# Spreading a layernorm's factors with one rounded product on a diagonal of blocks, in a local-attention feed-forward

## The chip, the cores and the metric

The kernel runs on one core of a Trainium2 chip, as one program. The metric is device time in microseconds of one execution; runs of the same kernel on the chip give a median. Engines are named as in the profile: PE multiplies matrices (PEld is its loading of weights), DVE is the vector engine, ACT the scalar engine, POOL the GpSimd engine, and SP issues the transfers. Each engine works through its own instructions in order and waits at semaphores for the others.

## The reference

The reference is a chain of eight blocks with residuals on x of 8 x 256 x 128 (batch, tokens, features): a state-space block, a local transformer, a softmax attention, the same local transformer again, a linear attention, a quantised feed-forward, a head attention, the quantised feed-forward. The change lies in the local transformer, which the kernel runs twice, six layers each time:

```python
for i in range(DEPTH):
    x = attn_layer(shift_tokens(x), Wqkv[i], q_scale[i], k_scale[i], Wo[i]) + x
    x = ffn_layer(shift_tokens(x), ln_g[i], ln_b[i], W1[i], b1[i], W2[i], b2[i]) + x

def ffn_layer(x, g, bln, W1, b1, W2, b2):
    mu = x.mean(-1, keepdims=True)
    var = ((x - mu) ** 2).mean(-1, keepdims=True)
    xn = (x - mu) / jnp.sqrt(var + 1e-05) * g + bln
    hg = xn @ W1 + b1
    a, gate = jnp.split(hg, 2, -1)
    return a * jax.nn.gelu(gate, approximate=False) @ W2 + b2
```

The attention has 16 heads of 64, windows of 32 tokens that look at themselves and the one before, l2-normed queries and keys, and rotary factors. The layernorm at the head of `ffn_layer` is what the change touches.

## The kernel before

Features lie on the 128 partitions and tokens along the free dimension. The batch is cut into four chunks of 512 tokens (two sequences of 256). A local-transformer stage (`LocalBlock`) has 6 layers x 4 chunks = 24 units; a unit goes through 8 steps, one for each pair of heads. `steps` writes out one order by hand for all engines, with the tile scheduler off: step i does, for several units at once, the part of each that is due. The names of a step, in the order in which they are issued:

- what the list `top` holds from the step before (small POOL subtractions of `split`, L203);
- `rotate`, POOL, two passes over 128x1024, L367 and L368, of the pair projected in the step before, after SP has swapped its halves;
- `prep`, PE L410 and twice DVE L414: the keys times their rounded factors `rs`;
- `attend`, PE L505, `share`, DVE L460 and L461, and `project`: PE `mm3` (L213 to L215), ACT copies L338 and squares L348, DVE L340;
- `rounded`, twice a unit: ACT L397, POOL L398, PE transposition L401, ACT L403; it makes the `rs` that the next step's `prep` multiplies by;
- `shared`, POOL L469; then weight loads that are due (`load_v` PE L283, `load_1` PE L296, ACT L298, DVE L299, L301);
- `norms` and `norms_end`: ACT L131 to L134, DVE L377, L142, L146, twice a unit;
- one piece of `feed`, the feed-forward of an older unit, in seven pieces and an eighth in the last step;
- `attended`, `turn` (PE L482, ACT L485), then what the list `mid` holds;
- `scores`: PE L429, then four DVE passes L437 to L440; `values`: PE L325, ACT L327; `squares`: PE L359; and `soft`: ACT's exponent L450, over the pair of scores that DVE has just finished, in odd steps.

The layernorm of `feed` is `layernorm_in_pieces`, cut over three steps. Piece one centres x with a matmul (L159), squares it (L161) and copies it (L163). Piece two sums the squares into `var`, where 32 rows of each quarter of the tile hold the variance of one quarter's 128 tokens (L167); ACT makes the first guess of the inverse root (L131, L132, L134), and `newton` is put on the list `mid`, so that DVE corrects it (L144, L146) later in the same step, ahead of that step's scores. Its result `y[0]` is 128x128: rows 32s to 32s+31 hold the factors of tokens 128s to 128s+127, all rows alike. Piece three, in the next step, spreads them over 128 partitions into the 128x512 bank `rb`, with four fp32 matmuls whose weights `one[:, s]` are 1 in row 32s and 0 elsewhere (L179); then DVE multiplies (L541). Each fp32 matmul appears in the trace as two records. Piece three falls into a step in which `rounded` runs too.

fp32r is fp32 rounded for a matmul of one pass; where full precision is needed, the kernel splits a value into a rounded part and the rounded rest (`split`, L203). Tiles of fp32r live in an arena of their own. PSUM has eight banks: five (RING) go round, and scores, norms and the attention's sum have one each.

Of the kernel before, what the change touches and what calls it, by code (L numbers as in the profile page):

```python
# [10 lines left out]
F32 = mybir.dt.float32  # L11
F32R = mybir.dt.float32r
BF = mybir.dt.bfloat16
AF = mybir.ActivationFunctionType
ALU = mybir.AluOpType
# [22 lines left out]
RING, SCO, NRM, ACC = "01234", "5", "6", "7"  # L38
# [5 lines left out]
def f32(ap):  # L44
    return ap.bitcast(F32)


class Arena:
# [3 lines left out]
    def __init__(self, big, at=0, end=SIZE, rounded=None):  # L52
        self.big, self.at, self.end, self.tags, self.rounded = big, at, end, {}, rounded
# [33 lines left out]
class K:  # L87
# [64 lines left out]
            pass  # L152
        return xs, rb

    def layernorm_in_pieces(self, pool, src, tags, sfx="", deep=2, mid=None):

        nc = self.nc
        xc = self.bank(tags[0])
        nc.tensor.matmul(xc, self.cmat, src, start=True, stop=True)  # L159
        sq = pool.tile([128, CT], F32, name="lnsq", tag="sq" + sfx, bufs=deep)  # L160
        nc.scalar.activation(sq, xc, AF.Square)  # L161
        xs = pool.tile([128, CT], F32, name="lnx", tag="fx" + sfx, bufs=deep)
        nc.scalar.activation(xs, xc, AF.Copy, scale=-0.5)  # L163
        yield xs, None
        var = self.bank(tags[1])
        for s in range(4):
            nc.tensor.matmul(var[32 * s:32 * s + 32, 0:128], self.ones32, sq[:, bass.ts(s, 128)],  # L167
                             start=True, stop=True)
        t = self.rsqrt_tables(pool, var, bias=self.eps, sfx=sfx)
        y = []  # L170
        newton = lambda: y.append(self.rsqrt_newton(pool, var, t, bias=self.eps, sfx=sfx))
        if mid is None:
            newton()
        else:
            mid.append(newton)
        yield xs, None
        rb = self.bank(tags[1])
        for s in range(4):
            nc.tensor.matmul(rb[:, bass.ts(s, 128)], self.one[:, s], y[0], start=True, stop=True)  # L179
        yield xs, rb  # L180

# [36 lines left out]
class LocalBlock:  # L218


    def __init__(self, k):
        self.k, self.nkb = k, 0
        nc = k.nc
        R = Arena(k.bigr, 0, RSIZE)
        self.P = P = Arena(k.big, k.con.at, SIZE, R)
        self.D = k.D
        self.mask = k.const(P, "c_mask", (128, 512), BF)
        self.hcol = k.const(P, "c_hcol", (128, 2))
        self.sel = k.const(P, "c_sel", (128, 2, GP, 32))
        bsel = P.tile([128, GP, 128], F32, name="c_bsel", tag="rr", bufs=1)  # L230
        nc.sync.dma_start(out=bsel, in_=k.a["c_bsel"])
        self.bsel = P.tile([128, GP, 128], F32R, name="bsel")
        nc.vector.tensor_copy(self.bsel, bsel)
        self.qs = k.const(P, "qs", (128, DEPTH, 4))
        self.ffc = k.const(P, "lngb", (128, DEPTH, 2))
        self.b2 = k.const(P, "b2", (128, DEPTH))
        self.b1 = k.const(P, "b1", (128, DEPTH, 6))
        self.zero = P.tile([32, 128], BF, name="zero")
        self.kb = [P.tile([128, 2, 32 + CT], F32, name="kb_%d" % i) for i in range(NKB)]
        self.y = [P.tile([128, 2, 257], F32, name="y_%d" % c) for c in range(NCH)]  # L240
        for t in [self.zero] + self.kb + self.y:
            nc.vector.memset(t, 0.0)

        for tag, n, bufs in (("fx", 512, 2), ("sq", 512, 3), ("lny", 128, 2), ("nwt128", 128, 2),
                             ("tab0", 512, 2), ("tab1", 512, 2), ("wr_64", 512, NWR), ("wr_128", 256, NWR),
                             ("wvo", 512, NWV), ("bias1", 8, 2), ("w2", 128, 3)):
            P.place(tag, n, bufs)
        for tag, n, bufs in (("xs", 1024, 2), ("wqk", 512, 9), ("w1", 256, 7), ("fh", 1024, 1), ("rs", 512, 2)):
            R.place(tag, n, bufs)

        self.rs, self.nrs = [P.tile([128, CT], F32R, name="rs", tag="rs") for _ in range(2)], 0
        for t in self.rs:
            nc.vector.tensor_scalar(t, self.mask, 0.0, None, ALU.mult)
# [280 lines left out]
    def feed(self, u):  # L534
        k, P, nc, w = self.k, self.P, self.k.nc, u.w
        assert u.att
        for xc, rb in k.layernorm_in_pieces(P, self.y[u.c][:, :, 0:256], (RING, RING), mid=self.mid):
            if rb is None:
                yield
        xn = P.tile([128, CT], F32, name="xn", tag="fx", bufs=2)  # L540
        nc.vector.tensor_tensor(xn, xc, rb, ALU.mult)  # L541
        yield
        xh = k.split(P, xn, (128, CT), "fh", 1, self.top)
        yield
        ge = P.tile([128, 3, CT], F32, name="ge", tag="ge", bufs=1)
        for i, m in enumerate((128, 128, 85)):
            gp = k.bank(RING)
            k.mm3(gp[:m], w.w1[3 + i], xh)
            nc.scalar.activation(ge[:m, i], gp[:m], AF.Gelu, bias=w.bias1[:m, 3 + i:4 + i])
        u.late = True  # L550
        yield
        yield
        hh = []
        for i, m in enumerate((128, 128, 85)):
            ap = k.bank(RING)
            k.mm3(ap[:m], w.w1[i], xh)
            nc.vector.scalar_tensor_tensor(ge[:m, i], ap[:m], w.bias1[:m, i:i + 1], ge[:m, i], ALU.add, ALU.mult)
            hh.append(ge[:m, i])
        yield
        acc = k.bank(RING)  # L560
        for i in range(3):
            m = (128, 128, 85)[i]
            nc.tensor.matmul(acc, w.w2[i][:m], hh[i], start=(i == 0), stop=(i == 2))
        self.residual(u.c, acc, self.b2[:, u.l:u.l + 1])
        yield
# [40 lines left out]

    def steps(self, us, ws, depth):
        NU, done, feed, side = len(us), [0] * NCH, None, []
        for i in range(-LEAD, 8 * NU + 20):
            def do(what, ahead):  # L610
# [26 lines left out]
            if 0 <= n < NU:  # L637
                u = us[n]
                last = u.l + 1 == depth
                if p == 0:  # L640
                    feed, fed = self.feed(u), u
                if p < 7:
                    next(feed)
# [856 lines left out]
```

## Time and profile before

| | before |
|---|---|
| runs, median (lowest to highest) | 4365.39 us (4363.03 to 4368.97), n = 3 |
| the profiled execution | 4360.81 us, span 4359.0 us, granted clock 0.926 |
| PE, DVE, ACT, POOL busy, share of the span | 87%, 85%, 60%, 71% |
| L179, PE | 480 records, 0.275 us each (median), all layernorms together |
| L367 and L368, POOL | 384 each, 2.39 us each |
| L437 to L440, DVE | 384 each, 0.69 to 0.70 us each |
| L450, ACT | 192, 1.06 us each |

How to read it: the page gives busy times over the whole span, the span in 40 slices, and groups of instructions by line. A window table gives busy times of a stretch, a timeline the instructions in order of time with start and duration, and in square brackets the idle time before an instruction and what ended it. An arrow `out<-in` names what is written and read: `big` and `bigr` are the two arenas in SBUF, `pb` is PSUM. Matmuls overlap in their pipe, so what one costs PE is read from the start of one to the start of the next. The local stages lie between some 690 and 2180 us and between 2470 and 3990 us; the state-space stage comes before, and attention stages between and behind.

### The profile page before, as it was taken

How to read it: one execution, taken by the hardware profiler on the slowest of the kernel's cores; microseconds unless marked ns; L12 is line 12 of the kernel's file. 1: busy time of each engine (PE TensorE's matmuls, PEld its weight loads, DVE VectorE, ACT ScalarE, POOL GpSimd, SP SyncE). 2: the span in 40 equal slices, each digit the busy share in tenths (PEclk: the TensorE clock that was granted, in tenths of full speed). 3: DMA queues.
4: the chain of work that ended last, by engine and by line, in shares of the span. 5: the costliest groups of instructions: out<-in, count | busy, mean ns of one | idle time of the engine just before them, and what ended most of it. 6: DMA issues, size and time to landing. Idle time of an engine off the chain costs nothing. (4 is left out here: it accounts for less than half of the span.)

```text
span 4359.0 us, 147963 instructions
## 1 busy us (share of the span) xinstructions
PE 3780.3 (87%) x64201; PEld 2852.4 (65%) x64201; DVE 3716.3 (85%) x5687; ACT 2628.5 (60%) x5050; POOL 3077.8 (71%) x1546
## 2 busy tenths in 40 slices
PE   5666679999999999999966899999999999998367
PEld 2222248777878778787744788787787877875144
DVE  6999958888888888888976788888888888897988
ACT  5433347777667676676645676676676767764322
POOL 3656668877778787787566887787787877872433
PEclk7777889999999999999977999999999999998578
DMA  0000023323233233232202332232323323321000
GB/s 19 7 3 16 1 77 78 91 73 89 73 74 89 71 89 76 71 93 71 63 22 67 81 92 74 69 94 72 89 70 76 87 71 90 75 72 47 15 6 10
DMA packets 134900, 272.98 MB, mean 63 GB/s; under 512 B 31020, under 2 KB 68328, under 8 KB 134248
## 3 DMA queue, kind: packets, MB, share of 16 engines
q1 hardware_dynamic: 134248, 263.51, 24.0%
q8 instruction: 504, 8.26, 0.8%
q14 instruction: 148, 1.21, 0.1%
HBM read 49.50 MB, written 6.29 MB: 13 GB/s over the span
## 5 line engine op out<-in xcount | busy, mean ns | idle before, releaser
L367 POOL TENSOR_TENSOR big<-big 128x1024 f32<-128x1024 f32 x384 | 915.8, 2385 | 466.7 <-DMA big<-big 322.6
L368 POOL TENSOR_TENSOR big<-big 128x1024 f32<-128x1024 f32 x384 | 916.5, 2387 | 30.1
L325 PE MATMUL pb<-big 128*32 128x128 f32 x24576 | 748.1, 274 | 2.7 <-DVE big L301 2.7
L325 PEld LDWEIGHTS pb<-big 128*32 128x32 f32 x24576 | 683.0, 111 | 8.5 <-DVE big L301 4.0
L327 ACT COPY big<-pb 128x512 f32<-128x512 f32 x768 | 439.4, 597 | 384.2 <-PE pb L325 381.0
L338 ACT COPY big<-pb 128x512 f32<-128x512 f32 x768 | 437.5, 587 | 276.8 <-PE pb L215 241.7
L414 DVE SCALAR_TENSOR_TENSOR big<-big,pb 128x512 f32<-128x512 f32 x768 | 536.0, 738 | 22.3 <-PE pb L410 22.0
L340 DVE TENSOR_TENSOR big<-pb,big 128x512 f32<-128x512 f32 x768 | 496.4, 677 | 58.6 <-ACT big L338 51.5
L213 PE MATMUL pb<-bigr 128*128 128x512 f32 (+1 forms) x1056 | 453.9, 430 | 9.8 <-DVE big L340 4.3
L469 POOL TENSOR_TENSOR big<-big 128x1024 f32<-128x1024 f32 x192 | 365.6, 1904 | 132.2 <-ACT big L338 54.8
L348 ACT ACTIVATE big<-big 128x512 f32<-128x512 f32 x768 | 444.2, 631 | 0.0
L821 POOL TENSOR_TENSOR big<-big 128x1024 f32<-128x1024 f32 x128 | 305.1, 2396 | 192.1 <-DVE big L820 187.1
L429 PE MATMUL pb<-big 128*32 128x128 f32 x12288 | 421.3, 278 | 6.0 <-DVE big L440 6.0
L215 PE MATMUL pb<-bigr 128*128 128x512 f32 (+1 forms) x1056 | 422.2, 400 | 4.6 <-DVE bigr L299 4.6
L214 PE MATMUL pb<-bigr 128*128 128x512 f32 (+1 forms) x1056 | 420.9, 399 | 1.1 <-POOL bigr L203 1.1
L429 PEld LDWEIGHTS pb<-big 128*32 128x32 f32 x12288 | 316.6, 110 | 142.2 <-issue 91.2
L437 DVE TENSOR_TENSOR pb<-pb,big 128x512 f32<-128x512 f32 x384 | 266.3, 694 | 144.2 <-PE pb L429 142.6
L505 PE MATMUL pb<-big 128*32 128x128 f32 x11520 | 377.9, 276 | 0.2 <-ACT big L485 0.2
L814 PE MATMUL pb<-bigr 128*128 128x512 f32 x512 | 216.1, 538 | 181.3 <-DVE big L820 125.7
L450 ACT ACTIVATE big<-big 128x1024 f32<-128x1024 f32 x192 | 203.7, 1061 | 263.6 <-DVE big L440 261.9
L505 PEld LDWEIGHTS pb<-big 128*32 128x32 f32 x11520 | 325.1, 110 | 48.0 <-issue 25.0
L816 ACT ACTIVATE big<-pb,big 128x1020 f32<-128x1020 f32 x128 | 142.2, 1111 | 282.0 <-PE pb L814 191.1
(270 smaller groups left out, 7450.7 us busy)
## 6 DMA issues: line engine op xcount, KB each, us to landing
big<-big SPq DMA_DIRECT2D x768, 256.0 KB, 3.6
big<-in_wqk SPq DMA_DIRECT2D x96, 128.0 KB, 3.5
big<-x SPq DMA_DIRECT2D x28, 256.0 KB, 2.7
big<-in_c_rot SPq DMA_DIRECT2D x24, 256.0 KB, 5.1
big<-in_wv SPq DMA_DIRECT2D x48, 128.0 KB, 3.6
big<-in_wo SPq DMA_DIRECT2D x48, 128.0 KB, 4.0
big<-big SPq DMA_DIRECT2D x384, 16.0 KB, 2.2
x<-big SPq DMA_DIRECT2D x20, 256.0 KB, 2.5
```

Of the source, the lines that this page charges most:

```text
L213: mm(out, w[:, 0], x[:, 0], start=start, stop=False)
L215: mm(out, w[:, 1], x[:, 0], start=False, stop=stop)
L325: nc.tensor.matmul(vp[32 * h:32 * h + 32, bass.ts(w, 128)], xw, wv[:, bass.ts(h, 128)], start=True, stop=True)
L327: nc.scalar.copy(v2[:, 4 * q:4 * q + 4].rearrange("p w f -> p (w f)"), vp)
L338: nc.scalar.copy(raw[:, s], ps)
L340: nc.vector.tensor_tensor(tt[:, s].rearrange("p (b t) -> p b t", b=2), ps.rearrange("p (b t) -> p b t", b=2), ct, ALU.mult)
L348: nc.scalar.activation(sq, raw[:, s], AF.Square)
L367: nc.gpsimd.tensor_tensor(s4, s4, u.w.tab[1][:, :, None, :].broadcast_to([128, 2, 2, T]), ALU.mult)
L368: nc.gpsimd.tensor_tensor(tt, tt, sw, ALU.add)
L414: nc.vector.scalar_tensor_tensor(kb[:, h, 32:], tt[:, 1], self.hcol[:, h:h + 1], rb, ALU.mult, ALU.mult)
L429: mm(s4[32 * w:32 * w + 32, 2 * wg:2 * wg + 2], qf[:, 32 * win:32 * win + 32], kb[:, :, 32 * win:32 * win + 64].rearrange("p h (o j) -> p ...
L505: mm(u.acc[32 * w:32 * w + 32, bass.ts(wg, 128)], pts[o][:, 32 * win:32 * win + 32], v2[:, win - 1 + o], start=False, stop=(g == 3 and o = ...
```

## The change

In the feed-forward's layernorm alone (`feed` passes `top`; other layernorms stay), the four fp32 matmuls L179 become one fp32r matmul over 512 columns. For that `newton`, on DVE, gets three more 128x128 passes: `hi` is the rounded `y[0]`; then `y[0]` is scaled by column 0 of `part` and has `hi` times column 1 added, so that row 32s holds the rounded value, row 32s+1 the rest, and the others 0. Four ACT copies, put on `top` and so issued at the head of the next step, write `y[0]` times column 2+s of `part` into quarter s of `z` (128x512, fp32r), which leaves two rows of each quarter: a diagonal of blocks. The weights `two` have 1 in rows 32s and 32s+1. The tiles `part` and `two` are set up once, with 26 small memsets and one cast on DVE. Line numbers below L179 move by 30 or less: in the changed kernel the three DVE passes are L179 to L181, the ACT copies L184, the new matmul L194.

```diff
+        def newton():
+            y.append(self.rsqrt_newton(pool, var, t, bias=self.eps, sfx=sfx))
+            if top is None:
+                return
+            hi = pool.tile([128, 128], F32R, name="lnh", tag="lnh")
+            nc.vector.tensor_copy(hi, y[0])
+            nc.vector.tensor_scalar(y[0], y[0], self.part[:, 0:1], None, ALU.mult)
+            nc.vector.scalar_tensor_tensor(y[0], f32(hi), self.part[:, 1:2], y[0], ALU.mult, ALU.add)
+            z = pool.tile([128, 4, 128], F32R, name="lnz", tag="lnz", bufs=2)
+            for s in range(4):
+                top.append(lambda s=s: nc.scalar.activation(z[:, s], y[0], AF.Copy, scale=self.part[:, 2 + s:3 + s]))
+            y.append(z.rearrange("p s t -> p (s t)"))
...
-        for s in range(4):
+        if top is not None:
+            nc.tensor.matmul(rb, self.two, y[1], start=True, stop=True)
+        for s in range(4 * (top is None)):
             nc.tensor.matmul(rb[:, bass.ts(s, 128)], self.one[:, s], y[0], start=True, stop=True)
...
+        two = P.tile([128, 128], F32, name="two", tag="rr", bufs=1)
+        nc.vector.memset(two, 0.0)
+        k.part = P.tile([128, 6], F32, name="part")
+        nc.vector.memset(k.part, 0.0)
+        for s in range(4):
+            nc.vector.memset(two[32 * s:32 * s + 2], 1.0)
+            nc.vector.memset(k.part[32 * s:32 * s + 2, 0:1], 1.0)
+            nc.vector.memset(k.part[32 * s:32 * s + 1, 0:1], 0.0)
...
+        k.two = P.tile([128, 128], F32R, name="two")
+        nc.vector.tensor_copy(k.two, two)
...
-        for xc, rb in k.layernorm_in_pieces(P, self.y[u.c][:, :, 0:256], (RING, RING), mid=self.mid):
+        for xc, rb in k.layernorm_in_pieces(P, self.y[u.c][:, :, 0:256], (RING, RING), mid=self.mid, top=self.top):
```

More of the change, by code (lines that the diff above doesn't have):

```diff
@@ L153, in layernorm, with layernorm_in_pieces @@
         return xs, rb
-    def layernorm_in_pieces(self, pool, src, tags, sfx="", deep=2, mid=None):
+    def layernorm_in_pieces(self, pool, src, tags, sfx="", deep=2, mid=None, top=None):
         nc = self.nc
@@ L170, in layernorm_in_pieces @@
         y = []
-        newton = lambda: y.append(self.rsqrt_newton(pool, var, t, bias=self.eps, sfx=sfx))
+        def newton():
[10 more added lines that the diff above has]
+            y.append(z.rearrange("p s t -> p (s t)"))
         if mid is None:
@@ L242, in __init__ @@
             nc.vector.memset(t, 0.0)
+        two = P.tile([128, 128], F32, name="two", tag="rr", bufs=1)
[6 more added lines that the diff above has]
+            nc.vector.memset(k.part[32 * s:32 * s + 1, 0:1], 0.0)
+            nc.vector.memset(k.part[32 * s:32 * s + 2, 1:2], -1.0)
+            nc.vector.memset(k.part[32 * s:32 * s + 1, 1:2], 1.0)
+            nc.vector.memset(k.part[32 * s:32 * s + 2, 2 + s:3 + s], 1.0)
+        k.two = P.tile([128, 128], F32R, name="two")
+        nc.vector.tensor_copy(k.two, two)
         for tag, n, bufs in (("fx", 512, 2), ("sq", 512, 3), ("lny", 128, 2), ("nwt128", 128, 2),
```

## The prediction

> **What bounds the kernel now.** I read the page's busy times, then the stage table (windows), then the timeline of all engines around one feed step.
>
> ```profile
> PE 3780.3 (87%) x64201; PEld 2852.4 (65%) x64201; DVE 3716.3 (85%) x5687; ACT 2628.5 (60%) x5050; POOL 3077.8 (71%) x1546
> ...
> PE   5666679999999999999966899999999999998367
> ```
> ```profile
> 1000.00:1900.00 900.00, 874.07 (x17339) 702.42 (x17340) 779.00 (x1233) 631.64 (x1205) 707.38 (x357) 1.00 0.33 81
> ```
>
> In 900 us of local attention PE is busy 874 us (97%) at the full clock, DVE 87%, POOL 79%, ACT 70%. Nearly all of PE's 26 idle us are waits for DVE or a late transfer. So in these two stages (about 690 to 3990 us) a microsecond taken from PE is won, and one in which PE stands is lost. The change acts in the step after the one where `newton` runs. An ordinary one, with chunk 3 in the feed-forward (timeline; start, duration):
>
> ```profile
> 1454.07 0.29 DVE L146 SCALAR_TENSOR_TENSOR big<-big,pb 128x128 f32<-128x128 f32 x1
> ...
> 1454.28 0.69 DVE L437 TENSOR_TENSOR pb<-pb,big 128x512 f32<-128x512 f32 x1
> ...
> 1455.10 2.38 POOL L367 TENSOR_TENSOR big<-big 128x1024 f32<-128x1024 f32 x1 [0.96 <-DMA big<-big]
> ...
> 1456.46 0.69 DVE L440 TENSOR_TENSOR big<-pb,big 128x512 f32<-128x512 f32 x1
> ...
> 1457.24 1.06 ACT L450 ACTIVATE big<-big 128x1024 f32<-128x1024 f32 x1 [1.65 <-DVE big L440]
> ...
> 1458.21 1.09 ACT L338 COPY big<-pb 128x512 f32<-128x512 f32 x2
> ...
> 1458.51 0.27 PE L401 MATMUL pb<-big 128*128 128x128 f32 x1
> 1458.62 1.06 PE L179 MATMUL pb<-big 128*128 128x128 f32 x8
> ...
> 1459.61 1.08 PE L429 MATMUL pb<-big 128*32 128x128 f32 x32
> ...
> 1460.98 1.28 POOL L398 TENSOR_TENSOR bigr<-big,bigr 32x512 fp32r<-32x512 f32 x1 [1.04 <-ACT big L403]
> ...
> 1462.80 0.50 PE L410 MATMUL pb<-bigr 128*128 128x512 f32 x1
> ```
>
> Call T the end of the layernorm's L146 (1454.36 here). PE has already finished this step's scores, so DVE is the late one: it goes straight from L146 to the scores' four passes (L437 to L440, done at T+2.79). ACT's exponent L450 has waited 1.65 us for them and ends at T+3.95. PE meanwhile is at prep, attend and projections, and reaches L179 at T+4.2 without a wait, since its operand is four microseconds old. The next scores start at T+5.25.
>
> **PE, removed and added.** L179 holds PE from 1458.62 to 1459.61, 1.0 us (1.1 in other feeds). One 128x512 fp32r matmul takes its place: such matmuls stand 0.23 us apart in a row (L213 to L215) and 0.33 to 0.43 us before another kind (L410). I take 0.38. Saved: some 0.65 us in each of 48 feeds, 31 us if nothing else moved.
>
> **DVE, added.** Three 128x128 passes between L146 and L437, each waiting for the one before. The 128x128 copy at L195 took 0.21 us; the shortest one-source scalar pass of that kind (L1168) 0.21; the nearest two-source pass is L299, 0.35 at its quick end. With 0.03 between them: d = 0.87 us if nothing blocks them.
>
> **ACT, added, and the new wait.** Four 128x128 scaled copies into fp32r. L1035, a 128x128 pass, lasts 0.39 and starts every 0.29, so four take about 1.27. They stand at the head of the next step, which on ACT's queue is behind L450, and L450 waits for L440. So z is complete at T + 3.95 + d + 1.18 (they may start 0.1 before L450 ends, as L338 does). The new matmul waits for z, and behind it on PE wait the next scores, values and everything else. New start of L429: T + 3.95 + 0.87 + 1.18 + 0.05 for the signal + 0.38 = T+6.43, against T+5.25 for chunks 0 and 3 (1.2 us lost), T+5.07 for chunk 1 (1.4 lost), and T+6.51 for chunk 2, where L283 stands ahead of L179 (0.1 won). 12 feeds of each: 14 + 16 + 14 - 1, about **+43 us**, the matmul's saving already in it. Bounds: if z were never late, -31; if the four copies ran end to end at 0.39, 0.35 more per feed, +17.
>
> **Behind it on ACT**: L338, L348, L397 and L403 run without gaps there, so all slip by d + 1.18 = 2.05, and so does POOL's L398, which makes the factors that the next step's first matmul L410 reads. L398 would end at T+9.95; L410, before at T+8.44, would come at T+9.6. Another 0.4 us in chunks 0, 1 and 3, 0.2 in chunk 2: **+16** (from 0 to 25). ACT has about 2.4 idle us a step, so that slip is gone in two steps.
>
> **Blocked by POOL.** Two instructions on SBUF alone do not pass each other on DVE and POOL in this trace. L299's shortest run is 0.31 us, its median 1.1, and it ends 0.1 to 0.15 us after the POOL instruction that it met. Two such passes in a row show it best:
>
> ```profile
> 2101.82 2.38 POOL L367 TENSOR_TENSOR big<-big 128x1024 f32<-128x1024 f32 x1 [3.98 <-PE pb L429]
> ...
> 2102.39 5.13 DVE L587 TENSOR_TENSOR big<-big 64x512 f32<-64x512 f32 x2
> ...
> 2104.28 2.69 POOL L368 TENSOR_TENSOR big<-big 128x1024 f32<-128x1024 f32 x1
> ```
>
> Two passes of 0.67 us each took 5.13: the first until L367 ended, the second until L368 did. L146 and the scores' passes have a PSUM operand and run through. The three new passes have none. One-source passes are held too: L692 takes 0.28 us, and 0.81 where it met POOL. I went through the 46 feeds that have scores behind them: in 20 POOL is idle at T and L367 comes only at T+0.6 to T+1.1 or later, when the last pass has begun, so d stays 0.87. In 26 (nine of chunk 0, where L299 had made T late, all twelve of chunk 1 with its L203, five of chunk 3) an L367, L368 or L203 is running, and another often follows at once. Letting DVE and POOL alternate as above gives d between 1.0 and 6.1 there, 2.7 more than free on average: 26 x 2.7 = **+70 us**. Bounds: +8 by the same table if only the two-source pass is held, 0 if the phases shift clear of POOL; all 35 feeds of chunks 0, 1 and 3 at 3.5 more, +123. I take 70, by L587 and L692.
>
> The Trainium skill (VectorE: DVE Perf Modes, the perf-mode tier table; SBUF — State Buffer, two separate sides) says that fp32 copies and scalar passes in SBUF run at twice the rate by taking both read ports, and then lock POOL out or wait for its whole instruction, as two-input passes do. L692 agrees for the scalar pass; no run here shows the 128x128 copy against POOL. By the rule all three passes alternate with POOL, and the sum would be the one below; without it for the copy and the scalar pass the sum would be some 60 us less.
>
> **Once, at the start**: 27 small memsets and copies on DVE during the state-space stage, where DVE is busy 500 of 560 us. At 0.06 us for one (L112), 2 us. The instruction order there and in the stage between shifts a little; I give that 5 us either way. **Given back**: feeds of chunks 0 and 1 already have 2 to 5 us in which PE waits for a late DVE; a PE that was held for z finds DVE less late. I take -8 (0 to -25).
>
> **Sum**: 43 + 16 + 70 + 2 - 8 = 123. The profiled execution took 4360.8 us (span 4359.0); its sum is 4484. The median of the runs is 4.6 higher, inside the noise of this term, so I forecast 4484, 2.8% slower.
>
> **Rivals.**
> 1. *The saving wins.* If L450 or the copies were done by T+4.2, PE would have its 0.65 us each time: 4361 - 31 = 4330. That needs DVE to have a slack of 2 us at T, and L437 starting right behind L146 with PE's scores 1.8 us old speaks against it. It decides as soon as z is ready before L401 ends. Chance 5%.
> 2. *Only the wait.* POOL's instructions shift so that the three passes fall into gaps, or the one-source passes are not held: 4361 + 43 + 16 + 2 + (0 to 8) - 8, 4414 to 4422. For it: PE's new stalls move DVE's and POOL's phases every feed. Chance 22%.
> 3. *More collisions.* DVE delayed, POOL's rotations bunch up, and the free feeds collide too: up to 4361 + 43 + 16 + 123, about 4543. For it: POOL is 79% busy and L367 comes only 0.75 us after T in many free feeds. Chance 13%.
> 4. *Gain and loss cancel*, PE waiting 0.65 us each time: 4361. Chance 3%. The forecast itself, 4430 to 4520: 57%.
>
> **How the numbers follow.** About 0.2% is what a measurement of this kernel can tell from no change. Faster is rival 1 (0.05), the same is rival 4 (0.03), all the rest is slower (0.92). The range runs from rival 2, with 10 us for the shifted order, to just short of rival 3's end: 4405 to 4535.
>
> **What would show it.** Right: a group of 48 matmuls at the new line with an idle time before it of 1 to 5 us, released by ACT's scaled copies, 80 to 150 us in all, PE's share in local attention down by 2 to 3 points. Right on the collisions: the three DVE lines with medians over their minima of 0.2 to 0.35 us and maxima near 2.4. Wrong: no idle time ahead of the new matmul (rival 1), or DVE lines all at their minima (rival 2). Idle PE ahead of L410 released by L398 would confirm the 16.

## The result, and the profile after

The changed kernel takes 4517.47 us (median of 4 runs, 4509.65 to 4534.91) against 4364.21 us for the kernel before: ratio 1.0357, 95% interval [1.0339, 1.0376]. The profiled execution took 4523.8 us, span 4522.0, granted clock 0.912 (before 0.926). The forecast was 4484 us with a range to 4535; by medians the change costs 153 us where the sum said 123.

The page's busy times and PE's strip, after:

```profile
PE 3814.3 (84%) x63865; PEld 2850.4 (63%) x63865; DVE 3844.9 (85%) x5858; ACT 2679.3 (59%) x5242; POOL 3078.8 (68%) x1546
...
PE   5666679999999899999966899999999999987367
```

The window table of 1000 to 1900 us (after the times: busy us of PE, PEld, DVE, ACT and POOL, then granted clock, DMA share, GB/s):

```profile
1000.00:1900.00 900.00, 828.72 (x16168) 659.53 (x16169) 777.73 (x1204) 606.35 (x1181) 661.71 (x332) 0.97 0.31 74
```

In the same 900 us PE is busy 829 us, 92%, instead of 874, and its clock is 0.97 instead of 1.00: there is less work done in the window, and some of it runs slower. DVE is as busy as it was, since its new passes fill what the slower pace leaves.

PE's waits after (us in total, times, longest):

```profile
PE pb L194 <- ACT bigr L184: 149.7, 48, 8.7
...
PE pb L440 <- POOL bigr L428: 18.2, 28, 5.6
```

The new matmul L194 waits in each of its 48 executions, always for the copies L184. Prep's matmul (L440, before L410) waits for POOL in 28 cases where it was 8; the added ones are short, about 0.2 us each. Before, the line was:

```profile
PE pb L410 <- POOL bigr L398: 15.5, 8, 6.9
```

A feed of chunk 1 shows how the wait comes about (timeline; all lines after moved by 30, so scores are L467 to L470 on DVE, the exponent L480, the rotation L397 and L398):

```profile
1072.72 0.29 DVE L146 SCALAR_TENSOR_TENSOR big<-big,pb 128x128 f32<-128x128 f32 x1
...
1073.05 0.73 DVE L179 CAST bigr<-big 128x128 fp32r<-128x128 f32 x1
...
1073.81 2.50 DVE L180 TENSOR_SCALAR big<-big 128x128 f32<-128x128 f32 x1
1073.84 2.38 POOL L397 TENSOR_TENSOR big<-big 128x1024 f32<-128x1024 f32 x1 [0.15 <-DVE bigr L179]
...
1076.30 2.36 POOL L398 TENSOR_TENSOR big<-big 128x1024 f32<-128x1024 f32 x1
1076.35 2.46 DVE L181 SCALAR_TENSOR_TENSOR big<-bigr,big 128x128 f32<-128x128 f32 x1
...
1078.73 0.69 DVE L467 TENSOR_TENSOR pb<-pb,big 128x512 f32<-128x512 f32 x1
...
1081.69 1.06 ACT L480 ACTIVATE big<-big 128x1024 f32<-128x1024 f32 x1 [7.44 <-DVE big L470]
1082.66 1.26 ACT L184 ACTIVATE bigr<-big 128x128 fp32r<-128x128 f32 x4
...
1083.97 0.80 PE L194 MATMUL pb<-bigr 128*128 128x512 f32 x1 [6.74 <-ACT bigr L184]
...
1084.70 1.94 PE L459 MATMUL pb<-big 128*32 128x128 f32 x32
```

A scaled pass over 128x128 (L180) takes 2.50 us and ends with POOL's L397; L181 ends just after L398. The scores' first pass L467 starts 5.7 us after T (the end of L146) instead of 0.89 as in a feed that meets no POOL instruction (before, it started 0.08 ahead of T), and the exponent, the copies, the matmul and the scores follow in a chain. PE stands 6.74 us. Over all 48 layernorms the three passes lasted (shortest, median and longest, in ns, behind the count):

```profile
L179 DVE CAST bigr<-big x48: 216/294/2382, 728.7 to 4167.1; 128x128 fp32r<-128x128 f32 x48
L180 DVE TENSOR_SCALAR big<-big x48: 274/288/2502, 729.0 to 4168.6; 128x128 f32<-128x128 f32 x48
L181 DVE SCALAR_TENSOR_TENSOR big<-bigr,big x48: 336/351/2544, 729.3 to 4169.7; 128x128 f32<-128x128 f32 x48
```

Behind PE's stand the scores L459 last 1.94 us where they took 1.08 before. That was not in the forecast; the window table of these microseconds shows why:

```profile
1075.00:1080.00 5.00, 2.24 (x24) 1.45 (x16) 4.93 (x4) 0.00 (x0) 3.58 (x2) 1.00 0.03 7
1080.00:1087.00 7.00, 3.03 (x49) 2.44 (x53) 6.44 (x11) 5.11 (x12) 0.45 (x1) 0.51 0.14 31
1087.00:1090.00 3.00, 3.00 (x81) 2.62 (x70) 2.90 (x5) 1.69 (x3) 2.92 (x3) 1.00 0.90 232
```

The granted clock fell to 0.50 at 1080.08, in the stand, for 6.83 us, and so past its end. In the local stages, all 22 stands of PE of 4 us or more are followed or met by such a drop of 3.41 or 6.83 us; of the 18 between 1.5 and 3 us only 6 are. But 4 us are no threshold: the kernel before has no such stand there, and 8 of its 12 stands between 1.5 and 3 us met a drop of 3.41 us.

A yardstick for what follows: I call **stretch** the time from a feed's first score pass on DVE (L437 before) to the next feed's. The last one of each local stage ends at the stage's last first pass. There are 46 in the local stages, of one chunk each; a feed's own wait for z lies in its own stretch, and the next feed's DVE passes lie in it too. Sums of stretches by chunk, in us, from the profiled executions (the names are those of the experiments below):

| | chunk 0 | chunk 1 | chunk 2 | chunk 3 | sum |
|---|---|---|---|---|---|
| before | 830.2 | 779.1 | 662.7 | 652.5 | 2924.5 |
| after | 882.2 | 824.7 | 676.7 | 702.9 | 3086.5 |
| e1, DVE passes alone | 860.8 | 788.7 | 670.7 | 687.6 | 3007.8 |
| e2, ACT copies alone | 844.0 | 791.5 | 662.2 | 661.5 | 2959.2 |
| e3, matmul alone | 825.8 | 776.5 | 657.0 | 650.3 | 2909.6 |
| e5, early copies | 861.4 | 790.5 | 667.5 | 690.9 | 3010.3 |
| e9, filled stand of chunk 1 | 872.3 | 808.7 | 673.4 | 707.6 | 3062.0 |
| e10, both remedies, ring turned | 838.8 | 790.1 | 662.1 | 660.1 | 2951.1 |
| e11, the same with two passes | 838.5 | 787.3 | 659.3 | 657.6 | 2942.7 |

The stretches hold 162 us of the 163 by which the span grew: all of the loss is in the two local stages.

### The profile page after: what moved, and what is told of

Same layout as the page of the kernel before. It is cut to its first block, busy times and chain, and to the rows that moved or that the text cites. A ratio compares the mean times of both kernels' runs of the same rounds, so it can differ in the third digit from the quotient of the medians.

```text
span 4522.0 us, 147661 instructions
## 1 busy us (share of the span) xinstructions
PE 3814.3 (84%) x63865; PEld 2850.4 (63%) x63865; DVE 3844.9 (85%) x5858; ACT 2679.3 (59%) x5242; POOL 3078.8 (68%) x1546
## 4 chain that ended last, share of the span: by engine, by line
PE 44%; DVE 30%; ACT 14%; issue 7%; POOL 4%; DMA 2%; SPq 0%; POOLq 0%; ACTq 0%; DVEq 0%
PE pb L355 8%; PE pb L459 5%; PE pb L535 5%; DVE big L850 4%; PE pb L230 4%; PE pb L232 3%; PE pb L231 3%; PE pb L593 3%; ACT big L368 2%; ACT big L378 2%; PE pb L389 2%; PE pb L440 2%; DVE big L370 2%; PE pb L512 2%; DVE pb L468 2%
## 5 line engine op out<-in xcount | busy, mean ns | idle before, releaser
L397 POOL TENSOR_TENSOR big<-big 128x1024 f32<-128x1024 f32 x384 | 915.6, 2384 | 467.9 <-DMA big<-big 287.6
L398 POOL TENSOR_TENSOR big<-big 128x1024 f32<-128x1024 f32 x384 | 916.1, 2386 | 30.1
L355 PE MATMUL pb<-big 128*32 128x128 f32 x24576 | 769.7, 279 | 4.1 <-DVE big L331 3.9
L355 PEld LDWEIGHTS pb<-big 128*32 128x32 f32 x24576 | 704.0, 113 | 13.2 <-DVE big L331 6.1
L357 ACT COPY big<-pb 128x512 f32<-128x512 f32 x768 | 438.3, 596 | 384.1 <-PE pb L355 381.8
L444 DVE SCALAR_TENSOR_TENSOR big<-big,pb 128x512 f32<-128x512 f32 x768 | 536.1, 739 | 30.1 <-PE pb L440 29.9
L459 PE MATMUL pb<-big 128*32 128x128 f32 x12288 | 438.6, 286 | 9.9 <-DVE big L470 9.7
L480 ACT ACTIVATE big<-big 128x1024 f32<-128x1024 f32 x192 | 203.8, 1061 | 382.0 <-DVE big L470 380.2
L459 PEld LDWEIGHTS pb<-big 128*32 128x32 f32 x12288 | 328.5, 114 | 156.8 <-issue 95.1
L467 DVE TENSOR_TENSOR pb<-pb,big 128x512 f32<-128x512 f32 x384 | 266.7, 694 | 155.8 <-PE pb L459 154.0
L535 PE MATMUL pb<-big 128*32 128x128 f32 x11520 | 379.6, 276 | 0.5 <-issue 0.3
L535 PEld LDWEIGHTS pb<-big 128*32 128x32 f32 x11520 | 325.9, 110 | 49.5 <-issue 26.8
```

The lines of the kernel that those rows point to most:

```text
L355: nc.tensor.matmul(vp[32 * h:32 * h + 32, bass.ts(w, 128)], xw, wv[:, bass.ts(h, 128)], start=True, stop=True)
L397: nc.gpsimd.tensor_tensor(s4, s4, u.w.tab[1][:, :, None, :].broadcast_to([128, 2, 2, T]), ALU.mult)
L398: nc.gpsimd.tensor_tensor(tt, tt, sw, ALU.add)
L444: nc.vector.scalar_tensor_tensor(kb[:, h, 32:], tt[:, 1], self.hcol[:, h:h + 1], rb, ALU.mult, ALU.mult)
L459: mm(s4[32 * w:32 * w + 32, 2 * wg:2 * wg + 2], qf[:, 32 * win:32 * win + 32], kb[:, :, 32 * win:32 * win + 64].rearrange("p h (o j) -> p ...
L535: mm(u.acc[32 * w:32 * w + 32, bass.ts(wg, 128)], pts[o][:, 32 * win:32 * win + 32], v2[:, win - 1 + o], start=False, stop=(g == 3 and o = ...
```

## Experiments: the parts alone

The theory was that of the forecast: DVE's three passes held up by POOL, and the matmul's wait for z behind the exponent, which stands on ACT's queue ahead of the copies. Each part was first put into the kernel alone. Two rivals: the parts cost their own length only, and the saving on PE is lost in other waits.

**e1: the three DVE passes alone**, their results used by nobody; the old four matmuls stay.

```diff
-            nc.vector.tensor_scalar(y[0], y[0], self.part[:, 0:1], None, ALU.mult)
-            nc.vector.scalar_tensor_tensor(y[0], f32(hi), self.part[:, 1:2], y[0], ALU.mult, ALU.add)
+            w = pool.tile([128, 128], F32, name="lnt", tag="lnt")
+            nc.vector.tensor_scalar(w, y[0], self.part[:, 0:1], None, ALU.mult)
+            nc.vector.scalar_tensor_tensor(w, f32(hi), self.part[:, 1:2], w, ALU.mult, ALU.add)
```

> Of the change only the three DVE passes are left: they write into tiles that nobody reads, and the four fp32 matmuls spread the factors as before. Lock theory: a pass on SBUF alone waits for POOL's whole instruction, so in about 25 of 46 feeds the scores' passes come 3 to 6 us late and PE waits for the next keys; the free feeds stay inside DVE's slack of 1.1 us. Before + 66 us + some 10 us of lowered clock after long stands: about 4440 (4415 to 4465), the three lines with maxima near 2.4 us. Rival, mere length: three passes of 0.3 us lie inside the slack, 4364 to 4372, and no maximum above 0.5.

Measured: 4449.33 us, ratio 1.0193 [1.0177, 1.0208], against 4363.02 in the same series. More than half of the change's loss comes from three passes of 0.2 to 0.35 us that nobody waits for but DVE's own queue.

**e2: the four ACT copies alone**, at the head of the next step, reading the factors that are there; results unused.

```diff
-            hi = pool.tile([128, 128], F32R, name="lnh", tag="lnh")
-            nc.vector.tensor_copy(hi, y[0])
-            nc.vector.tensor_scalar(y[0], y[0], self.part[:, 0:1], None, ALU.mult)
-            nc.vector.scalar_tensor_tensor(y[0], f32(hi), self.part[:, 1:2], y[0], ALU.mult, ALU.add)
...
-            y.append(z.rearrange("p s t -> p (s t)"))
```

> Of the change only ACT's four copies at the head of the step are left, of the factors as they are; nobody reads them, and the four fp32 matmuls stay. Theory: everything behind them on ACT slips by 1.2 us, POOL's L398 ends some 0.6 us behind the time at which the next prep matmul wants it, in 36 of 48 feeds: about 4384 (4370 to 4400), seen as idle PE ahead of that matmul. Rival: ACT is 60% busy and takes them up, 4364.

Measured: 4398.66 us, ratio 1.0077 [1.0062, 1.0092], at the upper end of the theory: 36 us. Here prep's matmul is L433, and in PE's waits it has the place in which it had 15.5 us in 8 times before:

```profile
PE pb L433 <- POOL bigr L421: 34.1, 41, 6.2
```

That is the chain of the knock-on term (ACT late, then POOL's L398, then prep), without any wait for z. It makes 19 of the 36 us.

**e3: the matmul alone**, over a tile of constant zeros. No passes, no copies; the factors are left out, so the kernel does not compute the reference's outputs.

```diff
-            nc.tensor.matmul(rb, self.two, y[1], start=True, stop=True)
+            nc.tensor.matmul(rb, self.two, self.zc, start=True, stop=True)
```

> Of the change only the matmul is left: one fp32r matmul over a constant tile takes the place of the four fp32 ones; no passes, no copies. It leaves out the factors (the spread values are zero), so the outputs are not the reference's. Theory: PE wins 0.65 us in each of 48 feeds, about 4333 (4325 to 4342). Rival: the step is bound by DVE, so that PE's saving turns into waits for it, 4355 to 4364.

Measured: 4357.71 us, ratio 0.9987 [0.9978, 0.9997]: 5 us, not 31. The rival was right. (The first feed comes 4 us later in it, its first score pass at 732.7 against 728.6; why was not tried.) The next scores do start about 0.65 us earlier (chunk 2: 5.9 us after the first score pass instead of 6.6), but the stretches shrink by 15 us in all. Waits of PE in that kernel, prep's DVE passes being L438 and the turn L506:

```profile
PE pb L383 <- DVE big L146: 40.3, 53, 3.3
...
PE pb L506 <- DVE big L438: 21.7, 14, 2.3
PE pb L434 <- POOL bigr L422: 17.0, 22, 5.8
```

Before, the same three took 35.0, 20.9 and 15.5 us. An earlier PE waits for DVE and POOL a little later on.

The parts alone add up to 86 + 36 - 5 = 117 of the 153 us. What is missing arises only together: the wait for z exists in none of the three.

## Experiments: the collisions and the order on ACT

**e4: the whole change, with the factors in PSUM**, in the columns of `var` from which newton read, so that each of the three passes has a PSUM operand, as L146 and the score passes have.

```diff
+            v, g = var[:, 0:128], var[:, 128:256]
+            nc.vector.scalar_tensor_tensor(t, v, self.eps, t, ALU.add, ALU.mult)
+            nc.vector.scalar_tensor_tensor(v, t, -3.0, g, ALU.add, ALU.mult)
...
-            nc.vector.tensor_copy(hi, y[0])
+            nc.vector.tensor_copy(hi, v)
```

> The whole change, but the factors stay in PSUM until the last pass, so that each of the three DVE passes has one PSUM operand, as L146 has. Lock theory: none waits for POOL, d is about 1.1 us in all feeds, the wait for z stays (1.8 us ahead of the new matmul in chunks 0, 1 and 3): 4517 - 70 - about 25 of lowered clock = 4425 (4405 to 4445). Rival, mere length: the passes are as long as before or a little longer, 4510 to 4525.

Measured: 4445.82 us, ratio 1.019 [1.0171, 1.0208]. 70 us of the loss go (153 lost against 83), as much as the forecast had for the collisions; the rival (no POOL lock) falls. The further 25 us that the expectation put on the lowered clock did not come, and the time is 1 us above what I had allowed. Two waits of PE show what is left, the new matmul (L198) for the copies, and one that this kernel brings itself, prep (L444) for the third new pass L185, because it needs the bank of `var`:

```profile
PE pb L198 <- ACT bigr L188: 52.5, 35, 8.5
...
PE pb L444 <- DVE big L185: 34.2, 44, 1.1
```

**e5: the whole change, with the copies issued by `newton` itself**, ahead of the exponent on ACT's queue; the passes stay in SBUF.

```diff
-                top.append(lambda s=s: nc.scalar.activation(z[:, s], y[0], AF.Copy, scale=self.part[:, 2 + s:3 + s]))
+                nc.scalar.activation(z[:, s], y[0], AF.Copy, scale=self.part[:, 2 + s:3 + s])
```

> The whole change, with the four ACT copies issued right behind the DVE passes of newton, so that on ACT's queue they stand ahead of that step's copies of the values and of the exponent, not behind them; the DVE passes still work in SBUF alone. Theory: of the 153 us that the change costs, some 59 are the matmul's wait for z behind the exponent (what is left when the collisions, about 82, and the small parts are taken off), and they come from the order on ACT's queue. z is then complete at about T + 0.9 + 1.3, two microseconds before PE comes to the matmul, in every feed that meets no POOL instruction; in the others the delayed scores alone remain, as in the kernel with the three passes only (1.0193). Expected 4445 us, 4425 to 4465, and hardly any idle time ahead of the new matmul. Rival: what costs is ACT's load, not its order; the copies then hold up the exponent and the copies of the values in their turn, and the time stays at 4510 to 4525.

Measured: 4460.53 us, ratio 1.0219 [1.0202, 1.0236], inside the expected range and well below the rival's. The new matmul's wait for the copies, 149.7 us after, is down to one case in the layernorm that has no scores behind it:

```profile
PE pb L431 <- ACT big L357: 37.8, 20, 3.2
PE pb L194 <- DVE big L444: 14.2, 10, 1.5
PE pb L194 <- ACT bigr L184: 8.7, 1, 8.7
```

But the first line is new: where the DVE passes collide, the copies now hold up ACT's copies of the values (L357) and with them the transposition L431. So the order on ACT is worth 55 us (153 lost against 98), and part of the wait only changes its owner.

**e6: both remedies in one** (edits of e4 and e5 together).

> Both remedies in one: the factors stay in PSUM so that each DVE pass has an operand there, and the ACT copies stand ahead of the exponent. Theory (two separate costs, the passes that POOL holds and the wait behind the exponent): both go, what stays is 0.9 to 1.0 us of DVE time in each feed, of which PE's earlier start of the next scores pays back up to 0.65: 4375 us, 4360 to 4390. Rival: the two costs are one, in that any delay of the scores on DVE is handed on to ACT, POOL and PE in turn; the kernel with PSUM operands then keeps most of its loss, 4410 to 4445.

Measured: 4397.82 us, ratio 1.0082 [1.007, 1.0094]. Most of both costs goes, against the rival's 4410 and more, but 35 us stay instead of 12, 8 us above the theory's range. I took prep's wait for L185 (34.4 us, 44 times, as in e4) for the rest, and tried twice to take it away.

**e8: the factors in the spare columns of the norms' bank.**

```diff
-            v, g = var[:, 0:128], var[:, 128:256]
+            v, g = self.bank(NRM)[:, 256:384], var[:, 128:256]
```

> As the kernel with both remedies, but the factors lie in columns 256 to 511 of the norms' bank, which nothing else uses, and not in the bank of var. Theory: of the 35 us that the kernel with both remedies still loses, nearly all is its own doing, namely prep's matmul in the same step, which takes the ring bank of var and waited there for the third DVE pass (34 us in 44 times); with that bank given up at newton's end as before, what remains is some 0.97 us of DVE time a feed, met by a matmul that is 0.65 us shorter: 4366 us, 4355 to 4380, no clear difference from before. Rival: what remains is DVE's later scores, which reach PE whatever the bank: 4385 to 4400.

Measured: 4438.76 us, ratio 1.0171 [1.0153, 1.0189]. Both expectations missed. The wait moved to a matmul that stands earlier in the step, that of the squares (L393), which writes other columns of the same bank and yet waits for the pass:

```profile
PE pb L393 <- DVE big L185: 62.3, 43, 2.7
```

**e10: e6, with the ring of banks turned on by one ahead of prep**, so that prep gets the bank of `turn`.

```diff
+            top.append(lambda: self.bank(RING))
```

> As the kernel with both remedies (PSUM operands in the bank of var, early copies), but the ring of five banks is turned on by one ahead of the next step's prep, so that prep takes the bank of turn, which ACT has emptied by then, and not the bank of var, which DVE's third new pass still reads. Theory: the 34 us of prep's wait for that pass (44 times) are nearly the whole of the 35 us that this kernel still loses; in the kernel with the norms' bank the same wait only moved to the squares' matmul, which stands still earlier on PE (62 us in 43 times). Without it: 4366 us, 4355 to 4385, and no group in which PE waits for the new passes. Rival: DVE's 0.97 us a feed reach PE by another wait (the bank of the values' copies, the turn's wait for prep's DVE passes): 4385 to 4405.

Measured: 4402.17 us, ratio 1.009 [1.0076, 1.0104]. The wait for L185 is gone, and nothing is won. The rival was right, in the time and in that another wait takes over: the values' matmuls (L360) now wait for the bank that DVE's rotary products (L375) read.

```profile
PE pb L360 <- DVE big L375: 24.6, 44, 0.9
PE pb L445 <- POOL bigr L433: 20.5, 32, 6.4
```

In e6 that wait is 3.9 us in 8 cases; so the turned ring, like e8's bank, mostly moved the wait to another pair, and what DVE's time alone costs cannot be read from e10.

**e11: e10 with two passes instead of three.** ACT's copy rounds anyway, so row 32s can hold the unrounded value.

```diff
-            nc.vector.tensor_scalar(v, v, self.part[:, 0:1], None, ALU.mult)
...
-            nc.vector.memset(k.part[32 * s:32 * s + 1, 1:2], 1.0)
+            nc.vector.memset(k.part[32 * s:32 * s + 1, 1:2], 0.0)
```

> As the kernel with the ring turned on, with one DVE pass less: ACT's copy into fp32r rounds anyway, so row 32s may hold the unrounded value; y becomes hi times a column (0 in row 32s, -1 in row 32s + 1) plus the value in PSUM, and the pass with column 0 of part goes. DVE's addition falls from 0.97 to some 0.60 us in each feed. If what is left after the turned ring is DVE's own time, 10 to 18 us less than that kernel: 4352 us, 4340 to 4370, that is level with the kernel before or just below it. Rival: DVE's time there is covered, and both kernels take the same time within 4 us.

Measured: 4385.93 us, ratio 1.0052 [1.0038, 1.0066]. The absolute number is above the range, since e10 was; the difference of 16 us lies in the 10 to 18 expected. The pass that went (L184, third column its mean in ns) had this row in e10:

```profile
L184 DVE TENSOR_SCALAR pb<-pb,big 128x128 f32<-128x128 f32 x48 | 16.7, 349 | 0.0
```

By the medians 16.7 us of DVE's time bought 16 us of the program's. By the stretches it bought 8 (2951.1 to 2942.7); the profiled execution of e11, 4392.75 us, was its slowest. So between half and all of DVE's time at this place is uncovered. Some 9 us show in the wait that the turned ring made, 24.6 us in e10 and here:

```profile
PE pb L359 <- DVE big L374: 16.0, 33, 0.9
```

No kernel that computes the outputs beats the one before: e3's 5 us are the most that the shorter matmul gave, and each pass that its operand needs costs some 8 to 16.

## Experiments: the lowered clock

**e7: the whole change, with 48 small products ahead of the new matmul in chunks 0 and 1**, work that keeps PE busy while it would stand.

```diff
+            for i in range(self.warm):
+                nc.tensor.matmul(rb[:, 0:128], self.two, self.two, start=True, stop=True)
             nc.tensor.matmul(rb, self.two, y[1], start=True, stop=True)
...
+                k.warm = 48 if u.c < 2 else 0
```

> The whole change, and ahead of the new matmul 48 products of the weights tile with itself (128 columns each, fp32r, into the first quarter of rb, which the matmul then overwrites) in the feeds of chunks 0 and 1, the ones that mostly meet POOL. They are some 3 us of work that waits for nothing, in the place where PE otherwise stands 4 to 7 us for z. Theory (a stand of about 4 us or more lowers the granted clock to 0.50 for 3.4 or 6.8 us, which costs some 10 to 25 us in all): most of the 30 lowered stretches in the two local stages go, the clock there comes back to 0.99, and although PE has more to do the time falls to 4500, 4490 to 4510. Rival (the clock follows something else, or work at half clock is hidden behind DVE anyway): no gain, 4515 to 4540.

Measured: 4587.27 us, ratio 1.0508 [1.0484, 1.0531]. As a whole this went wrong, and the trace says where. The products took 5.55 us at full clock, not 3. In ten feeds of chunk 0 they had to wait for the bank `rb`, which prep's DVE pass L446 still read; PE then stood 1 to 5 us first and did the products at a granted clock of 0.50 to 0.64, in 8.4 to 10.5 us:

```profile
PE pb L195 <- DVE big L446: 36.0, 10, 5.1
```

Chunk 0 took 70 us more than after (952.4). In chunk 1 the filling waited for nothing, and its stretches took 809.8 us instead of 824.7, although the matmul came later. That half was repeated by itself.

**e9: the filling in chunk 1 alone**, with 40 products.

```diff
-                k.warm = 48 if u.c < 2 else 0
+                k.warm = 40 * (u.c == 1)
```

> As the kernel with 48 filling products, but 40 of them (some 4.6 us by that kernel's trace) and in the feeds of chunk 1 alone, where the filling waited for nothing. Theory (a PE that stands 4 us or more runs at half clock afterwards): the twelve stretches of chunk 1 show no lowered clock, take some 15 us less than the 824.7 of the changed kernel, and the other chunks stay as they are: 4502 us, 4495 to 4510. Rival (the clock costs nothing, since what is slowed waits for DVE anyway): 4512 to 4525 and the same length of chunk 1.

Measured: 4507.48 us, ratio 1.0335 [1.0318, 1.0352]; the profiled span is 4504.7. The interval overlaps that of the changed kernel (1.0357 [1.0339, 1.0376]), so the program's time alone would not prove it. The stretches do: chunk 1 has 2 lowered segments instead of 14, and takes 808.7 us instead of 824.7, 16 us less, with more work in it (e7, 809.8). Chunk 0, where nothing is filled and which was to stay as it was, is 10 us shorter as well. The clock is not the cause there (30.7 us of lost clock, the sum of the missing share over time, in both): its stretches hold the DVE passes of chunk 1's feeds, and POOL held these up by 25.4 us here, by 34.4 after. Chunk 1's own stretches hold chunk 2's passes, which met POOL in neither kernel, so its 16 us are free of that. One feed of chunk 1, first in the changed kernel:

```profile
1643.00:1648.00 5.00, 0.43 (x3) 0.07 (x1) 4.90 (x8) 1.83 (x4) 2.47 (x2) 0.87 0.01 3
1648.00:1655.00 7.00, 6.55 (x115) 5.56 (x116) 5.46 (x10) 4.69 (x12) 3.85 (x3) 0.61 0.53 135
```

and the same feed in e9:

```profile
1628.00:1634.00 6.00, 6.00 (x91) 5.40 (x90) 5.83 (x10) 2.98 (x8) 4.87 (x3) 1.00 0.06 13
1634.00:1641.00 7.00, 7.00 (x139) 6.34 (x139) 5.78 (x11) 4.80 (x12) 4.28 (x4) 1.00 0.51 133
```

PE busy throughout keeps a clock of 1.00 (the column after POOL's); PE that stood five microseconds has 0.61 in the seven that follow.

## Why the prediction was right, and where it was short

The direction, the place and the mechanisms were right, and the time lay in the range; the sum was 30 us short by the medians, and 40 by the profiled executions (163).

- **Wait for z: right.** In feeds that meet no POOL instruction the next scores start at T+6.57 (forecast T+6.43), with 1.76 us of idle time ahead of L194 in chunks 0 and 3 and 0.67 in chunk 2. e5 shows that the order on ACT's queue makes it. (The bound for copies end to end is 4 x 0.39 - 1.27 = 0.29 us a feed, +14, not +17.) PE's share in the window of local attention fell by five points, not by two to three.
- **Collisions: right in number and size.** The time from T to the first score pass exceeds 0.89 us in 25 feeds (forecast 26), by 70 us in all (forecast 70). The one-source passes L179 and L180 are held too, as the longest durations of 2.4 and 2.5 us above show. e4 takes 70 us off. The second choice, only the two-source pass held (8 us), is refuted by L180 above.
- **Knock-on: right in the step, cheap in the sum.** In chunk 3 prep's matmul comes at T+10.05 instead of T+8.44, as the terms said (1.2 + 0.4), but its wait for POOL grew from 15.5 us to 18.2 only, against 16 forecast. e2 shows the chain by itself, at 19 us.
- **Setup: nothing.** T of the first feed lies at 728.7 us in both. Of 2 us that says little: e1, with the same setup, has 731.5.
- **The step that failed is the first: "a microsecond taken from PE is won", with DVE at 87% taken for the engine that has room.** What failed on it is the saving of 31 us (e3: 5 in medians, 15 in the stretches); the -8 "given back" no run shows by itself. The sentence holds in chunk 2, whose full stretches last 64.1 us before and 63.5 in e3 (medians), the whole 0.65; in chunk 0 a part is won (4.4 of 7.8 us), and the stretches of chunks 1 and 3 shrink by 0.2 and 0.1 (66.7 to 66.5, 65.6 to 65.5). What DVE is given goes the same way: e1's three passes, which put off the scores by 0.84 us where they meet no POOL instruction, lengthen chunk 1's stretches by 0.6 us (to 67.3) and leave chunk 2's at 64.1. Beyond that room every microsecond is paid: the changed kernel's chunk 2 has 64.8 us where the next feed's passes meet no POOL instruction, and 65.4, 65.3 and 69.7 where they are held up by 0.44, 0.47 and 4.92 us. So DVE, 87% busy over the stage, has 0.8 us of room in some steps and 0.3 or less in others.
- **Left out: the clock.** Stands of 4 to 7 us were in the forecast, and what PE's clock does after them was not. e9 shows 16 us for chunk 1. The Trainium skill (TensorE: Matmul & The Clock Gate, Part 1: The HAM clock gate) would have said it: idle for a whole activity window of about 3.4 us, the array drops to half rate. The trace agrees in that each of 22 stands of 4 us or more has a segment of 3.41 or 6.83 us at half clock; it shows such segments after stands of 1.5 to 3 us as well, which are shorter than that window (6 of 18, and 8 of 12 before). Chunk 0, with 13 such segments against 7 before, should have lost some 9 us in the same way, an estimate by chunk 1's 16 us for 32 us of lost clock (35.8 in the changed kernel, 3.4 in e9) and chunk 0's 19 (30.7, before 11.9); it could not be filled, since the bank is late there, and stays open.

The same loss as a chain of kernels, each with one thing less, by medians against the kernel before in the same series:

| step | us |
|---|---|
| matmul alone (e3) | -5 |
| + three DVE passes that POOL does not hold, copies early (e10) | 47 |
| + passes in SBUF, held by POOL (e5 against e10) | 56 |
| + copies behind the exponent, with what PE's stands cost in clock (after against e5) | 55 |
| sum | 153 |

Three passes at the 16 us of e11 would make 48, the second row; at the 8 of its stretches they make 25, so what the early copies and the turned ring add to that row is not settled. The shares depend on the order and on the partner: e4 takes the collisions away first and finds 70, e6 against e5, which differ in the PSUM operands alone, 63. In e10 and e11 some 13 us of the span lie outside the stretches: between the local stages (326.3 us before from the first one's last first score pass to the second one's first stretch, 333.1 and 335.4 then) and behind the second (379.5 before, 386.4 and 383.5). Why they grew was not tried.

## What to carry to other kernels

Where two engines are both near full in a stage, a trade from one to the other is worth the difference only if the receiving engine has room in that very step; price each added pass on it at its full length first, and ask what cover there is after. A pass on DVE with all operands in SBUF can cost as long as the POOL instruction that it meets (here 2.4 us for 0.2 to 0.35), and several in a row may each meet one; an operand in PSUM avoids that, but then the bank's next writer waits for the pass. When a forecast contains stands of PE, price the slower clock that follows them too.

## What the runs showed of the hardware

- A 128x128 cast in SBUF that takes 0.22 us alone took up to 2.38 beside a POOL instruction of 2.38; in PSUM it took 0.29 each time. Three such short passes in a row delayed DVE's queue by up to 5.9 us.
- In or after 22 of 22 stands of PE of 4 us or more the granted clock was 0.50 for 3.41 or 6.83 us (of shorter ones, 1.5 to 3 us, 6 of 18, and 8 of 12 before); while an array was kept busy with meaningless products it kept 1.00.
- A matmul into columns 0 to 127 of a PSUM bank waited for a DVE pass that read columns 256 to 383 of it (e8). Whether the chip or the kernel's own semaphores order them was not tried.
- Forty-eight fp32r products of 128 columns, each with its own weight load, took 5.55 us, 0.116 each, at full clock, and 10.5 where the granted clock was 0.50 throughout.
